# An SSM convolution and a 16-expert MoE in one kernel: coefficients computed between the steps of a series, loads and small VectorE work moved behind the first heads

## The chip, the cores and the metric

The kernel runs on one NeuronCore of a Trainium2 chip. The metric is the device time of one execution in microseconds (us); less is better. Three executions of the kernel before took 910.34, 914.94 and 912.26 us, so their median is 912.26 us. A further execution, the profiled one, gave every row that is quoted here.

## The reference, cut to what matters

`x` has shape (128, 32, 512): 128 batches, 32 heads `h`, 512 positions `l`. A diagonal state-space model with 64 states per head gives each head a convolution kernel:

```
dt = exp(log_dt);  A = -exp(log_A_real) + i*A_imag;  dtA = A*dt
Ct = C * (exp(dtA) - 1) / A
K[h, l] = 2 * Re( sum_n Ct[h, n] * exp(dtA[h, n] * l) )
y = (causal convolution of x with K over l) + x*D, set to 0 where l >= length[batch]
```

`y` has 4096 rows (batch, head) of 512. A router (sigmoid of a 16-column product, plus bias) takes 4 of 16 experts for each row. Each expert is a gated unit, `silu(y Wg) * (y Wu)` times `Wd`, with 256 inner columns; a shared expert of the same size works on every row. The output is `x` plus all of it.

## The kernel before, in words

**The head of the program.** Everything begins with `Ct` and the waves `exp(dtA*l)`. `exp_into` (L273) makes `dn = exp(logs)`, that is `dt` and `nar = exp(log_A_real)`, in 32 columns. `waves` (L303) makes the magnitude `mag` by a polynomial (`exp_parts`, L258: the six dependent steps of L269 are "the series") and cosine and sine on ScalarE, for one chunk of states. There are six chunks (`CHUNKS`, L281); (c0, n) covers heads 2*c0 to 2*(c0+n)-1. L342 to L374 then form `Ct` as `ct_r`, `ct_i` by small VectorE operations of 16 columns: `er + i*ei = exp(dtA) - 1` (L344 to L349), `C` times that (L353 to L358), divided by `A` (L361 to L374). `kernels` (L379) multiplies waves and `Ct` into factors (the last one is L403), lets TensorE turn them into a chunk's kernel rows (`pk`, L407), adds the skip term (`krow`, L415) and writes them to DRAM (`kd`, L421 and L422). `kernel_strip` (L427) reads them back as a Toeplitz matrix, the `strip` of a block of four heads, 1 MB.

**The convolutions.** `tb` numbers eight blocks of four heads. In the loop at L998 TensorE convolves head 0, head 1, and then two heads at a time (`convolve`, L602, products at L610), with x read as `xt` (1 MB a block, L155, two buffers). How much of the sequence the longest row lets it leave out is read from `skips` by TensorE's sequencer ahead of heads 2 and 3 (L625). VectorE masks each result into `yb` (L628), ScalarE's queue writes a block of `yb` to `y_rows` in DRAM (L1006), TensorE turns it into `yT` (L634). `behind_head` (L954) puts the other work behind each head: waves of chunk 1 and 2 after heads 0 and 1, kernels of chunk 1 after head 0, of chunk 2 after head 3, of chunk 3 after head 8. The router's `gates`, `sums` and `route` follow each block or second block.

**Order.** In this stage TensorE's order is the one written in the program; that of VectorE, ScalarE, GpSimd and of the SyncE queue (which issues nearly all loads) is found by the scheduler from priorities and dependencies, `dep(a, b)` adding a dependency by hand. Ahead of head 0 TensorE runs eight matmuls that only keep it busy (L446), the ranking of rows by length (L496, L498, from `longer`, L493), and eight more; `rank`, `to_rank` and `to_row` (L503 to L508) are read from that PSUM result.

**From 121 us on** every engine's order is written in the program. Eight units run through the shared expert (`w_sh`, the last 3072 columns of `store`; L1071, L1086), then tiles of routed rows through the experts (L1211, L1237). Behind the last unit's third `down`, `registers(0)` and `registers(1)` (L1148, L1149) load two registers each on TensorE (L1202, L1205).

Of the kernel before, what the change touches and what calls it, by code (L numbers as in the profile page):

```python
# [28 lines left out]
F32 = mybir.dt.float32  # L29
BF16 = mybir.dt.bfloat16  # L30
F16 = mybir.dt.float16
I32 = mybir.dt.int32
AF = mybir.ActivationFunctionType
ALU = mybir.AluOpType
# [4 lines left out]
P = 128  # L39
# [17 lines left out]
AHEAD = 4  # L57
NT = (B * H * TOPK - E) // P + E
NT_MIN = B * H * TOPK // P
LAST_DRAIN = NT_MIN - 4  # L60
TS = 64
SKIPS = 4
# [17 lines left out]
def ssm_moe_kernel(  # L80
# [71 lines left out]

    def load_xt(tb):
        t = xp.tile([P, KT, HB, P], F32, tag="x", name=f"xt{tb}")
        nc.sync.dma_start(out=t, in_=x_t[tb])  # L155
        return t

    def dep(of, on, why):
# [88 lines left out]
    def ptile(name):  # L247
        return const.tile([P, NC2], F32, tag=name, name=name)

    def reduce_angle(r, k):  # L250
# [4 lines left out]
            nc.vector.scalar_tensor_tensor(r, k, -part, r, ALU.mult, ALU.add)  # L255
        nc.vector.tensor_scalar(r, r, -math.pi, math.pi, ALU.max, ALU.min)

    def exp_parts(v, q, k, s):  # L258

        nc.vector.tensor_scalar(v, v, -87.0, 88.0, ALU.max, ALU.min)
        nc.vector.tensor_scalar(k, v, 1.0 / math.log(2.0), ROUND, ALU.mult, ALU.add)
        nc.vector.tensor_scalar(k, k, ROUND, None, ALU.subtract)
        for part in (LN2_1, LN2_2):
            nc.vector.scalar_tensor_tensor(v, k, -part, v, ALU.mult, ALU.add)
        nc.vector.tensor_scalar(q, v, SERIES[0], None, ALU.mult)
        for c in SERIES[1:]:
            nc.vector.scalar_tensor_tensor(q, q, c, v, ALU.add, ALU.mult)  # L269

        nc.vector.tensor_scalar(s, k, 127.0, 2.0**23, ALU.add, ALU.mult)
# [67 lines left out]

    first, (mag, q, s, r, half) = waves(*CHUNKS[0], NC2)  # L340

    t0, t1, t2, t3 = (ptile(f"t{i}") for i in range(4))  # L342
    ex, em1, er, ei = mag[:, :NC2], ptile("em1"), ptile("er"), ptile("ei")
    nc.vector.tensor_mul(t1, q[:, :NC2], s[:, :NC2])  # L344
# [3 lines left out]
    nc.vector.tensor_add(er, t0, em1)  # L348
    nc.vector.tensor_mul(ei, ex, r[:, :NC2])  # L349

    c_r, c_i = cc[:, 0, :], cc[:, 1, :]
    nr, ni = ptile("nr"), ptile("ni")
    nc.vector.tensor_mul(t0, c_r, er)  # L353
    nc.vector.tensor_mul(t1, c_i, ei)
    nc.vector.tensor_sub(nr, t0, t1)
    nc.vector.tensor_mul(t0, c_r, ei)
    nc.vector.tensor_mul(t1, c_i, er)
    nc.vector.tensor_add(ni, t0, t1)  # L358

    rd, m0, m1 = ptile("rd"), ptile("m0"), ptile("m1")  # L360
    nc.vector.tensor_mul(m0, nar, nar)  # L361
    nc.vector.tensor_mul(m1, aim, aim)
    nc.vector.tensor_add(m0, m0, m1)
    nc.vector.reciprocal(rd, m0)
    nc.vector.tensor_mul(t0, ni, aim)
    nc.vector.tensor_mul(t1, nr, nar)
    nc.vector.tensor_sub(t0, t0, t1)
    nc.vector.tensor_mul(t2, ni, nar)
    nc.vector.tensor_mul(t3, nr, aim)
    nc.vector.tensor_add(t2, t2, t3)  # L370

    ct_r, ct_i = ptile("ct_r"), ptile("ct_i")
    nc.vector.scalar_tensor_tensor(ct_r, t0, 2.0, rd, ALU.mult, ALU.mult)
    nc.vector.scalar_tensor_tensor(ct_i, t2, 2.0, rd, ALU.mult, ALU.mult)  # L374


    kd_of, strip = {}, {}

    def kernels(c0, n, mag, cos, sin):  # L379

# [19 lines left out]
        nc.vector.tensor_add(g_r, g_r, g_t)  # L400
        nc.vector.tensor_mul(g_i, e_r, by_i)
        other.tensor_mul(e_i, e_i, by_r)
        nc.vector.tensor_sub(g_i, g_i, e_i)  # L403
        pk = ps_m.tile([P, n, 2 * LB], F32, tag="m", name=f"pk{c0}")
        for c in range(n):
            for g, f in ((g_r, f_r), (g_i, f_i)):
# [17 lines left out]
            kd_of[h] = kd[h - 2 * c0 : h - 2 * c0 + 1, :]  # L424
        return last

    def kernel_strip(tb):  # L427
        s = ks1.tile([P, HB, L], F32, tag="strip", name=f"strip{tb}", bufs=2)

        each = 1 if tb == 0 else HB  # L430
        for q in range(0, HB, each):
            kd = kd_of[tb * HB + q]
            nc.sync.dma_start(
                out=s[:, q : q + each, :],
                in_=bass.AP(kd.tensor, kd.offset, [[1, P], [PAD + L, each], [1, L]]),
            )
        strip[tb] = s

# [35 lines left out]


    len_col = const.tile([P, 1], F32, tag="len_col", name="len_col")
    behind(nc.vector.tensor_copy(len_col, len_col_i))
    key_row = const.tile([P, B], F32, tag="key_row", name="key_row")
    behind(nc.vector.tensor_copy(key_row, len_row_i))
    key_col = const.tile([P, 1], F32, tag="key_col", name="key_col")  # L480
    longest = const.tile([1, 1], F32, tag="longest", name="longest")
    for key, raw, own in ((key_row, key_row, cpos), (key_col, len_col, ppos)):
        nc.vector.tensor_scalar(key, raw, 0.0, float(L), ALU.max, ALU.min)
        if key is key_row:
            nc.vector.tensor_reduce(longest, key[0:1, :], AX.X, ALU.max)
        if key is key_col:
            num_len = const.tile([P, 2], F16, tag="num_len", name="num_len")
            behind(nc.vector.tensor_copy(num_len[:, 0:1], ppos))
            nc.vector.tensor_copy(num_len[:, 1:2], key)
        nc.vector.scalar_tensor_tensor(key, key, float(P), own, ALU.mult, ALU.subtract)  # L490

    longer = const.tile([P, B], BF16, tag="longer", name="longer")
    nc.vector.tensor_scalar(longer, key_row, key_col, None, ALU.is_lt)  # L493
# [10 lines left out]

    to_rank = const.tile([P, P], F32, tag="to_rank", name="to_rank")
    nc.vector.tensor_scalar(to_rank, cpos, rank, None, ALU.is_equal)
    to_row = const.tile([P, P], F32, tag="to_row", name="to_row")
    nc.vector.tensor_scalar(to_row, rank_ps[:, :B], ppos, None, ALU.is_equal)  # L508

    of_ranks = {}  # L510

    def ranks():
# [3 lines left out]
        def later(op):  # L516
            dep(op, last_mask, "later in VectorE's order")

        to_rank_h = const.tile([P, P], F16, tag="to_rank_h", name="to_rank_h")
        later(nc.vector.tensor_copy(to_rank_h, to_rank))  # L520
        unit = const.tile([P, NU], BF16, tag="unit", name="unit")
        later(nc.vector.tensor_scalar(unit, upos, 0.0, None, ALU.is_equal))

# [53 lines left out]


    skips = const.tile([1, 1], I32, tag="skips", name="skips")
    nc.vector.tensor_scalar(longest, longest, -1.0, float(L), ALU.mult, ALU.add)  # L580
    floor_div(longest, longest, TS)
    nc.vector.tensor_scalar(skips, longest, float(SKIPS - 1), None, ALU.min)


    within = const.tile([P, L], F32, tag="within", name="within")
# [363 lines left out]
    weights_at = {19: 0, 27: 1}  # L949
    made_waves, strips, k_us = {}, [1], {}  # L950
    ybs, xbs, rest_of_ranks = {}, {0: load_xt(0)}, ranks()
    nc.sync.dma_start(out=w_sh, in_=w_all[E])

    def behind_head(h):  # L954

        tb, q = divmod(h, HB)
        if h in waves_at:
            made_waves[waves_at[h]] = waves(*waves_at[h], 0)[0]
        if h in kernels_at:
            c = kernels_at[h]  # L960
            chunk_last[c[0]] = kernels(*c, *made_waves[c])
            behind_masks(chunk_last[c[0]])

        if strips[-1] in (tb, tb + 1) and strips[-1] < NB and strips[-1] * HB in kd_of:
            kernel_strip(strips[-1])
            strips.append(strips[-1] + 1)
        if h in (22, 25, 29):
            next(rest_of_ranks, None)
        if h in weights_at:
            weights_out(weights_at[h])  # L970
        if q == 2 and tb > 0:
            gates(tb - 1)
        last = h == H - 1
        for each in turns_at(h):
            turn_y(each, ybs[each // HB])
        if q == 3 and tb > 0 and not last:
            sums_and_route(tb - 1)
        if last:

            sums_and_route(tb - 1)  # L980
            k_us[0] = nc.tensor.value_load(of_ranks["k_u"][0:1, 0:1], min_val=1, max_val=KT)
            turned = turn_y(h, ybs[tb])
            gates(tb)
            return turned
# [12 lines left out]
    with tc.manual_schedule(engines={mybir.EngineType.PE}):  # L997
        for h, n in [(0, 1), (1, 1), *((h, 2) for h in range(2, H, 2))]:  # L998
            tb, q = divmod(h, HB)
            if q == 0:  # L1000
                ybs[tb] = yp.tile([P, HB, L], F32, tag="yb", name=f"yb{tb}")
                if tb + 1 < NB:
                    xbs[tb + 1] = load_xt(tb + 1)
            convolve(tb, range(q, q + n), xbs[tb], ybs[tb])
            if q + n == HB:
                nc.scalar.dma_start(out=y_bh[:, tb * HB : (tb + 1) * HB, :L], in_=ybs[tb])  # L1006
            for each in range(h, h + n):
                turned = behind_head(each)

# [106 lines left out]
    def unit_step(u):  # L1116
# [20 lines left out]
        for q in range(TU // P):  # L1137
            if u > 0 and not (u == NU and q == TU // P - 1):
                down(u - 1, q)
                if q % 2 == 1:  # L1140
                    next(making, None)
                if q == 0 and u + 1 < NU:
                    unit_register(u + 1)
            if u == NU - 1 and q == TU // P - 2:
                for _ in making:
                    pass

                registers(0)  # L1148
                registers(1)  # L1149
                registered = True  # L1150
        while "get" in made and gathered < AHEAD:
            gather(gathered)
            gathered += 1
# [225 lines left out]
```

## Time and profile before

| | us |
|---|---|
| median of three runs | 912.26 |
| the profiled execution | 913.3 |
| span of its core, first to last instruction | 911.5 |
| around the span (the difference) | 1.8 |
| TensorE busy | 871.8 |
| VectorE busy | 414.5 |
| first product of head 0 | 23.11 |
| first matmul of the shared expert | 121.53 |
| first routed product | 268.23 |

A row of the timeline has the start, the duration, the engine (PE is TensorE, PEld its weight load, DVE VectorE, ACT ScalarE, POOL GpSimd, SPq and ACTq the DMA-issuing queues), the line, the operation, what is written from what, and in brackets how long the engine sat idle before it and what released it. The chain of waits is the path that ended last: start, length, who. A row of a window has its length, the busy time of PE, PEld, DVE, ACT and POOL with their counts, then the granted TensorE clock (1.00 is full), the busy share of the DMA engines and their GB/s. A span of an operation on VectorE is longer than the distance to the next one where the two overlap; the chain shows the distance.

### The profile page before, as it was taken

The page shows a single profiled execution, that of the slowest core. Times are in us where ns is not written, and L with a number is a line of the kernel's source. Part 1 is how long each engine was busy: PE and PEld are TensorE (multiplying, and loading weights), DVE is VectorE, ACT ScalarE, POOL GpSimd, SP SyncE. Part 2 cuts the span into 40 slices and gives each one's busy share as a digit, 9 for nine tenths or more (in the row PEclk, how much of TensorE's full clock was granted, in tenths as well). Part 3 has the DMA queues.
Part 4 walks back from the last instruction along what each step waited for, and adds up shares of the span by engine and source line. Part 5 has one row for each costly group of instructions (what it writes and reads, how often), then busy time and mean ns, then how long its engine had stood idle before and what let it go on. Part 6 is the DMA issues. An engine that isn't in the chain of part 4 may idle for free.

```text
span 911.5 us, 14694 instructions
## 1 busy us (share of the span) xinstructions
PE 871.8 (96%) x2976; PEld 445.1 (49%) x2976; DVE 414.5 (45%) x1488; ACT 188.6 (21%) x379; POOL 421.7 (46%) x372
## 2 busy tenths in 40 slices
PE   2999999999999999999999999999999999999992
PEld 1667754444445444445444544444444554444440
DVE  8977774878712334323342334333333233344331
ACT  1222221112221122212221122112221111222220
POOL 2210012323574556555664556555654445566462
PEclk9999999999999999999999999999999999999997
DMA  5677586786696767666676667566765656677573
GB/s 200 211 269 257 198 276 181 220 179 163 101 218 168 179 118 130 132 165 118 120 138 169 110 117 138 111 106 118 133 115 99 107 107 107 110 139 132 106 131 75
DMA packets 54710, 136.03 MB, mean 149 GB/s; under 512 B 12432, under 2 KB 12592, under 8 KB 50992
## 3 DMA queue, kind: packets, MB, share of 16 engines
q0 software_dynamic: 36256, 89.77, 53.9%
q1 hardware_dynamic: 14096, 36.15, 11.3%
q10 hardware_dynamic: 4224, 8.39, 2.5%
q8 instruction: 76, 1.25, 0.5%
q14 instruction: 58, 0.48, 0.2%
HBM read 288.08 MB, written 60.64 MB: 383 GB/s over the span
## 4 chain that ended last, share of the span: by engine, by line
PE 91%; DVE 4%; DMA 1%; issue 1%; POOL 0%; ACT 0%; SPq 0%; DVEq 0%; ACTq 0%; POOLq 0%
PE g L1211 35%; PE o L1237 25%; PE py L610 6%; PE o L1086 5%; PE m L1179 5%; PE g L1071 4%; PE u L1071 4%; PE u L1229 3%; PE pt L634 1%; PE pa L901 1%; PE parts L655 1%; DMA strip<-kd 1%; PE pg L672 1%; DVE wq L269 0%; DVE pick L834 0%
## 5 line engine op out<-in xcount | busy, mean ns | idle before, releaser
L1211 PE MATMUL g<-store,yt 128*128 x742 | 342.9, 595 | 1.5 <-issue 1.1
L1247 POOL DMA_INDIRECT out<-ob,put x134 | 209.8, 1566 | 228.4 <-DVE junk L1186 204.1
L1237 PE MATMUL o<-store,zT 128*128 x536 | 252.0, 592 | 0.0
L1223 DVE SCALAR_TENSOR_TENSOR zt<-g,wt,sgt 128x256 f32<-128x256 f32 x135 | 65.3, 484 | 302.8 <-ACT sgt L1222 302.8
L1211 PEld LDWEIGHTS g<-store,yt 128*128 128x128 f32 x742 | 130.3, 190 | 118.2 <-issue 117.4
L1036 POOL DMA_INDIRECT yg<-y_rows,get x140 | 142.1, 1015 | 49.6 <-issue 38.6
L1237 PEld LDWEIGHTS o<-store,zT 128*128 128x128 f32 x536 | 101.5, 190 | 128.7 <-issue 124.1
L1246 DVE COPY ob<-o 128x512 f32<-128x512 f32 x134 | 92.7, 692 | 109.2 <-PE o L1237 100.2
L1185 ACT COPY yt<-m 128x512 f32<-128x512 f32 x136 | 79.6, 585 | 225.9 <-PE m L1179 219.7
L1222 ACT ACTIVATE sgt<-g 128x256 f32<-128x256 f32 x135 | 51.8, 383 | 267.2 <-PE g L1211 267.2
L1095 POOL DMA_INDIRECT out<-ob,unit_rows x32 | 50.0, 1563 | 93.0 <-ACT ob L1093 59.8
L1179 PEld LDWEIGHTS m<-ident,yg 128*128 128x128 f32 x373 | 48.7, 141 | 72.2 <-issue 71.7
L610 PE MATMUL py<-strip,xt 128*128 128x192 f32 (+7 forms) x256 | 63.6, 403 | 1.2 <-DMA strip<-kd 1.2
L1179 PE MATMUL m<-ident,yg 128*128 128x128 f32 x373 | 63.1, 273 | 0.8 <-issue 0.6
L1086 PE MATMUL o<-store,z 128*128 128x512 f32 x128 | 58.0, 597 | 0.7 <-ACT ob L1093 0.7
L1232 DVE COPY zT<-u 128x256 f32<-128x256 f32 x134 | 56.4, 421 | 1.3 <-PE u L1229 1.3
L610 PEld LDWEIGHTS py<-strip,xt 128*128 128x128 f32 x256 | 44.4, 195 | 19.6 <-issue 12.8
L1229 PE MATMUL u<-ident,zt 128*128 128x128 f32 x268 | 51.2, 273 | 0.0
L1071 PE MATMUL g<-store 128*128 128x512 f32 x92 | 42.8, 600 | 0.5 <-PE parts L655 0.3
L913 DVE TENSOR_SCALAR cols<-tpos_h,stl,tok 128x143 f16<-128x143 f16 x128 | 42.3, 336 | 0.0
L1071 PE MATMUL u<-store 128*128 128x512 f32 x92 | 42.2, 593 | 0.0
L1086 PEld LDWEIGHTS o<-store,z 128*128 128x128 f32 x128 | 23.4, 190 | 26.5 <-issue 24.9
(285 smaller groups left out, 493.1 us busy)
## 6 DMA issues: line engine op xcount, KB each, us to landing
store<-in_w_all SPq DMA_DIRECT2D x143, 1536.0 KB
xt<-in_x_t SPq DMA_DIRECT2D x8, 1024.0 KB
y_rows<-yb ACTq DMA_DIRECT2D x8, 1024.0 KB
out<-in_x POOLq DMA_DIRECT2D x8, 1024.0 KB, 15.7
strip<-kd SPq DMA_DIRECT2D x7, 1024.0 KB
yg<-y_rows,get POOLq DMA_INDIRECT x140, 4.4
out<-ob,put POOLq DMA_INDIRECT x134, 4.9
strip<-kd SPq DMA_DIRECT2D x4, 256.0 KB
```

The lines of the kernel that those rows point to most:

```text
L610: nc.tensor.matmul(py[:, c0 : L - jt * P], lhsT=xt[:, jt, q, :], rhs=strip[tb][:, q, jt * P + c0 :], start=(jt == 0), stop=(jt == KT - 1 o ...
L1036: nc.gpsimd.indirect_dma_start(out=at(yg, t), out_offset=None, in_=y_rows[:, :], in_offset=bass.IndirectOffsetOnAxis(ap=made["get"][:, t : ...
L1071: nc.tensor.matmul(ps[it], lhsT=w_sh[:, c0 : c0 + P], rhs=yT[:, u, kt, :, :].rearrange("p h b -> p (h b)"), start=(kt == KT - n), stop=(kt ...
L1086: nc.tensor.matmul(po, lhsT=at(zu, u)[:, it, q * P : (q + 1) * P], rhs=w_sh[:, c0 : c0 + L], start=(it == 0), stop=(it == IT - 1),)
L1179: nc.tensor.transpose(pt[:, q, :], at(yg, t)[:, q * P : (q + 1) * P], ident)
L1185: nc.scalar.copy(at(yt, t), pt)
L1211: mm = nc.tensor.matmul(pgu, lhsT=at(yt, t)[:, q, :], rhs=ring_flat[:, bass.ds(w0s[t] + q * 2 * I, 2 * I)], start=(q == KT - n), stop=(q = ...
L1223: nc.vector.scalar_tensor_tensor(at(zs, t), pgu[:, I:], at(wts, t), sg, ALU.mult, ALU.mult)
L1229: nc.tensor.transpose(at(p_z, t)[:, it, :], at(zs, t)[:, it * P : (it + 1) * P], ident)
L1237: mm = nc.tensor.matmul(po, lhsT=at(zts, t)[:, it, :], rhs=ring_flat[:, bass.ds(w0s[t] + WD + it * L, L)], start=(it == 0), stop=(it == IT ...
L1246: nc.vector.tensor_copy(ob, po)
L1247: add = nc.gpsimd.indirect_dma_start(out=out, out_offset=bass.IndirectOffsetOnAxis(ap=made["put"][:, t : t + 1], axis=0), in_=ob, in_offse ...
```

## The change

1. `Ct` is regrouped. The coefficient `ca` (2 C / A up to sign and conjugation: `ca_r`, `ca_i`) is formed from `nar`, `aim` and `cc` alone, by twelve operations that stand in the program between the first waves and `er`; three of them wait for the first operation of the waves' series, so that they and what follows from them fall among its steps. After `er` and `ei` six operations are left (four products, one sum, one difference).
2. The second block of x (`tb == 1`) waits for the last of block 0's four strip loads.
3. The shared expert's weights `w_sh` are no longer loaded (1.5 MB) at the start by SyncE's queue, but in six pieces of 256 KB on ScalarE's queue, each behind the y_rows write of blocks 1 to 6 and behind the same mask.
4. The length keys are formed in four operations instead of six, behind chunk 0's last factor (L403) instead of behind its `krow`; `num_len`'s two casts go to the first part of `ranks()` (behind head 22).
5. `skips` is found behind chunk 1's last factor.
6. `to_row` is no longer made from PSUM on the spot: ScalarE copies the rank row to SBUF and VectorE makes `to_row` behind head 10.
7. `registers(0)` goes behind the last unit's second `down`, `registers(1)` stays behind the third.

```
     def load_xt(tb):
...
+        load = nc.sync.dma_start(out=t, in_=x_t[tb])
+        if tb == 1:
+            dep(load, first_strips, "behind what is wanted first")
...
+    def between(op):
+        dep(op, in_series, "between the series' steps, of which each waits for the one ahead")
+
+    between(nc.vector.tensor_mul(m0, nar, nar))
+    nc.vector.tensor_mul(m1, aim, aim)
+    nc.vector.tensor_add(m0, m0, m1)
+    nc.vector.reciprocal(rd, m0)
+    nc.vector.tensor_mul(ca_r, c_i, aim)
+    between(nc.vector.tensor_mul(m1, c_r, nar))
+    between(nc.vector.tensor_mul(ca_i, c_i, nar))
+    nc.vector.tensor_mul(m2, c_r, aim)
+    nc.vector.tensor_sub(ca_r, ca_r, m1)
+    nc.vector.tensor_add(ca_i, ca_i, m2)
+    nc.vector.scalar_tensor_tensor(ca_r, ca_r, 2.0, rd, ALU.mult, ALU.mult)
+    nc.vector.scalar_tensor_tensor(ca_i, ca_i, 2.0, rd, ALU.mult, ALU.mult)
...
+    nc.vector.tensor_mul(t0, ca_r, er)
+    nc.vector.tensor_mul(t1, ca_i, ei)
+    nc.vector.tensor_mul(t2, ca_i, er)
+    nc.vector.tensor_mul(t3, ca_r, ei)
+    nc.vector.tensor_add(ct_r, t0, t1)
+    nc.vector.tensor_sub(ct_i, t2, t3)
...
+    for key, raw in ((len_col, len_col_i), (key_row, len_row_i)):
+        op = nc.vector.tensor_scalar(key, raw, 0.0, float(L), ALU.max, ALU.min)
+        dep(op, factors_last[0], "later in VectorE's order")
+    nc.vector.scalar_tensor_tensor(key_col, len_col, float(P), ppos, ALU.mult, ALU.subtract)
+    nc.vector.scalar_tensor_tensor(key_row, key_row, float(P), cpos, ALU.mult, ALU.subtract)
...
+    nc.scalar.copy(rank_row, rank_ps[:, :B])
     to_row = const.tile([P, P], F32, tag="to_row", name="to_row")
-    nc.vector.tensor_scalar(to_row, rank_ps[:, :B], ppos, None, ALU.is_equal)
...
+    def find_skips(after):
+
+        longest = const.tile([1, 1], F32, tag="longest", name="longest")
+        op = nc.vector.tensor_reduce(longest, key_row[0:1, :], AX.X, ALU.max)
+        dep(op, after, "later in VectorE's order")
+        nc.vector.tensor_scalar(longest, longest, -1.0, float(L * P), ALU.mult, ALU.add)
+        floor_div(longest, longest, TS * P)
+        nc.vector.tensor_scalar(skips, longest, float(SKIPS - 1), None, ALU.min)
...
-    nc.sync.dma_start(out=w_sh, in_=w_all[E])
+    first_strips = strip_loads[-1]
...
+            if h == 0:
+                find_skips(factors_last[c[0]])
...
+        if h == TO_ROW_AT:
+            to_row_op = nc.vector.tensor_scalar(to_row, rank_row, ppos, None, ALU.is_equal)
+            behind_masks(to_row_op)
...
                 nc.scalar.dma_start(out=y_bh[:, tb * HB : (tb + 1) * HB, :L], in_=ybs[tb])
+                if 1 <= tb <= PIECES:
+
+                    own = slice((tb - 1) * WSZ // PIECES, tb * WSZ // PIECES)
+                    load = nc.scalar.dma_start(out=w_sh[:, own], in_=w_all[E][:, own])
+                    dep(load, masks[-1], "behind what is wanted first")
...
-            if u == NU - 1 and q == TU // P - 2:
+            if u == NU - 1 and q in (1, 2):
                 for _ in making:
                     pass
 
-                registers(0)
-                registers(1)
-                registered = True
+                registers(q - 1)
+                registered = q == 2
```

`PIECES` is 6 and `TO_ROW_AT` is 10.

## The prediction, made before the changed kernel was built or run

> **What bounds the kernel now.** I read the page's busy row first, then the chain of waits, then the timelines of TensorE and of SyncE's queue for the stretch up to 121 us, then the half-second windows where TensorE stands still.
>
> ```profile
> PE 871.8 (96%) x2976; PEld 445.1 (49%) x2976; DVE 414.5 (45%) x1488; ACT 188.6 (21%) x379; POOL 421.7 (46%) x372
> ```
>
> TensorE is busy 96% of 911.5 us. From 268 us on it multiplies with hardly a gap, and the change touches nothing there. Of the 39.7 us without a matmul 16 lie ahead of the first one and some 15 behind the last, so only a few are left between. Where is it?
>
> ```profile
> 17.28 3.57 PE L446 MATMUL py<-ones 128*128 128x512 bf16 x8 [0.40 <-DVE krow L415]
> 23.11 2.32 PE L610 MATMUL py<-strip,xt 128*128 128x512 f32 x8
> 26.48 0.22 PE L407 MATMUL pk<-f_r,gg_r 128*32 128x32 f32 x2 [1.05 <-DVE gg_r L400]
> 34.08 0.25 PE L407 MATMUL pk<-f_r,gg_r 128*32 128x32 f32 x2 [0.71 <-DVE gg_r L400]
> 59.15 5.57 PE L610 MATMUL py<-strip,xt 128*128 128x448 f32 x16 [1.23 <-DMA strip<-kd]
> 260.39 1.98 PE L1086 MATMUL o<-store,z 128*128 128x512 f32 x4 [0.69 <-ACT ob L1093]
> ```
>
> TensorE's timeline: the first real work is at 15.96, the first product of head 0 at 23.11; then come four holes, of 1.05, 0.71, 1.23 and 0.69 us. Head 0 doesn't wait for its strip: the keep-busy matmuls and the ranking fill 17.28 to 23.11 and TensorE takes them in order. What starts them is `krow`, and the chain ahead of `krow` is VectorE alone, from 4.07 us on. In it the series looks like this (chain of waits; start, length):
>
> ```profile
> 11.11 0.29 DVE wq L269
> 11.39 0.02 issue
> 11.42 0.28 DVE wq L269
> 11.69 0.09 DVE t L346
> 11.78 0.23 DVE wq L269
> ```
>
> One step to the next takes 0.31 us (11.11 to 11.42). With a 16-column operation (L346) between two of them the timeline's next step starts at 11.73, again 0.31 later: the filler was free.
>
> **The change, part by part.** The sum is made against the profiled execution: 913.3 us, 911.5 of span and 1.8 around it, which is 1.0 above the median of 912.26.
>
> *`Ct` regrouped.* Eighteen operations before, eighteen after; only the place counts. (a) Ahead of the waves the chain has L361 0.09, L363 0.09, an issue of 0.02 and the reciprocal L364 0.25. All leave: -0.45. (b) Behind the series, from L344 (12.31) to the first factor L398 (15.32), stand 25 operations in 3.01 us, 0.12 each. Fourteen leave (L353 to L358, L365 to L370, L373, L374), six come: -8 x 0.12 = -0.96. (c) Nine operations go among the main series' steps; the other three depend on inputs alone and fit among the steps of `dn`'s series, as L362 does at 4.68. The main series has six gaps of 0.31 - 0.18 = 0.13 (0.18 is the distance from L266 to an operation that doesn't depend on it), two already taken by L271 and L346. Five find room there or behind the last step, four don't: 4 x 0.09 = +0.36, of which I take 0.30. Net -1.10.
> The Trainium skill speaks against (c): "VectorE: DVE Perf Modes", section "The DRAIN you can't avoid", says the next operation does not start until the pipe is empty, and so to cut the count of operations. By that each of the nine costs its 0.17 and 0.02 of issue, +1.7, and the whole is +0.3, a loss. The row at 11.69 differs (0.09 and no delay of the next step), so I take -1.10 and keep +0.3 as the other end.
>
> *Small VectorE work out of the stretch from `krow` to chunk 1's factors* (17.17 to 26.34). By start-to-start distance: casts L477 0.07 and L479 0.13, `num_len` 0.14, `to_row` 0.26 and the keys (L483, L490, L493) 0.68 leave it, the keys into the 0.62 in which VectorE waits for `pk`; skips' operations (L485 to L582) 0.46 go behind it. Together 1.7, more than the hole of 1.05 at 26.48. But VectorE also reads `rank` in this stretch (it stood 0.41 for it, L503), and that comes 3.7 behind the start of keep-busy whatever VectorE does; if the scheduler leaves `rank` at the same place in the order, up to 1.5 turns into waiting there and 0.2 is left. Ends -1.05 and -0.2; I take -0.8, since a scheduler that knows the wait can put series steps ahead of it. The hole of 0.71 at 34.08 stays: its factors follow head 1's mask (L628, 29.33), which moves with TensorE.
>
> *Moved work that I cost at nothing, with its cover.* `skips`: six operations, 1.1 us as a chain (0.20 and five of 0.18), behind chunk 1's factors; TensorE's sequencer wants it 2.2 behind the present factors, and a mask of 0.6 may come between: no margin to speak of, 0 to +0.5, taken 0. The rank row's copy on ScalarE: it idles 11.2 ahead of L329 at 22.17; behind it waits only that sine. `to_row` behind head 10: 0.26 among masks, wanted at 82. The six pieces: six issues of 0.37 to 0.42 on ScalarE's queue, each behind a y_rows issue with the same mask, so no new wait; behind them stand the yT copies (L635), with 3.4 to 6.8 of idle time in most rows. The sixth goes out near 111.7 and takes 0.7 at 370 GB/s; it is wanted at 121.5. Between 77 and 103 the DMA engines are full; there the mask of head 20 (89.06) waited 2.9 for a y_rows write and has 0.85 left until head 23 needs its PSUM: 0 to +0.7, taken 0. The 1.5 MB that vanish from the start (DMA full from 9 to 17.2) make `kd` and the strips up to 2 us earlier, but head 0 waits for the keep-busy matmuls: 0.
>
> *Registers.* One pair takes 1.3 us of TensorE's sequencer (257.6 to 258.9); two are 2.6 against the 1.72 of one `down`, hence the 0.69 at 260.39. Split, each lies behind a `down`: -0.65.
>
> Sum: 1.10 + 0.80 + 0.65 = 2.55. The strip hole stays: chunk 3's `pk` is not late (49.76, factors done at 45.8), and what follows (`kd` 50.96, strip 52.89, landed 59.1) moves as a whole. 912.26 - 2.55 = 909.7 us.
>
> **The rivals.**
>
> *R1, slower: x's second block is in the way of the second strip.* SyncE's queue shows what an x block does to the next small write:
>
> ```profile
> 28.98 0.39 SPq L433 DMA_DIRECT2D strip<-kd  x1
> 32.95 0.36 SPq L155 DMA_DIRECT2D xt<-in_x_t  x1
> 35.09 0.33 SPq L422 DMA_DIRECT2D kd<-krow  x1
> 39.73 0.37 SPq L433 DMA_DIRECT2D strip<-kd  x1
> ```
>
> `kd` was written in 1.42 at 27.56 (to 28.98), but in 4.64 at 35.09, two us behind an x block. After the change x's second block goes out near 22 and chunk 1's `kd` near 25.7. If that took 4.64, strip 1, which now lands near 34 with about 1.2 to spare, would come 2.0 too late at heads 4 and 5. And such a hole costs twice:
>
> ```profile
> 59.00:59.50 0.50, 0.35 (x1) 0.30 (x2) 0.47 (x4) 0.00 (x0) 0.43 (x1) 1.00 1.03 377
> 59.50:60.00 0.50, 0.50 (x2) 0.29 (x1) 0.47 (x2) 0.00 (x0) 0.37 (x2) 0.54 1.09 410
> 62.00:62.50 0.50, 0.50 (x5) 0.50 (x3) 0.50 (x4) 0.00 (x0) 0.00 (x0) 0.50 0.99 381
> 63.00:63.50 0.50, 0.50 (x2) 0.19 (x1) 0.35 (x2) 0.00 (x0) 0.00 (x0) 1.00 1.05 410
> ```
>
> Behind the 1.23 of idle time the granted clock is 0.50 for some 3.2 us, and sixteen matmuls take 5.57 instead of 3.62: +1.95. So 2.0 + 1.95 - 2.55 = +1.4: 913.7. It starts to cost when `kd` takes over 2.6 and cancels the gain at about 3.2. Against it: at 35.09 a strip's tail and a y_rows write (35.27) were under way as well, while from 24 to 30 the engines are idle (share 0.03), so that 1 MB at 420 GB/s is through by about 26.
>
> *R2: the gaps are not free* (the drain rule holds): +0.3 - 0.8 - 0.65 = -1.15: 911.1.
>
> *R3: `rank` takes the freed time*: -1.10 - 0.2 - 0.65 = -1.95: 910.3.
>
> *R4: the half clock falls away.* "TensorE: Matmul & The Clock Gate", part "The HAM clock gate", lets the clock fall after an idle window of about 3.4 us and calls the window free-running. Here 1.23 us of idle time sufficed, and 1.05 at 26.48 did not. If the place in such a window decides, a shift of 2 us can save the 1.95, or put it on another hole; by the page no hole of this size costs it at all. I keep it where it is, as the trace has it: -2.55 - 1.95 gives 907.8.
>
> *R5: the pieces or `skips` cost what I put at nothing*: +0.7: 910.4.
>
> **How the numbers follow.** Forecast 0.47, R1 0.12, R2 0.11, R3 0.11, R4 0.12, R5 0.07. Likeliest is 909.7; the cases span 907.8 to 913.7, and single runs of the kernel before scatter by 2.7 around their median, so the range is 907.0 to 913.5. What a measurement of this kernel can tell from no change is about 0.5%, 4.6 us. Faster by more (under 907.7) needs R4 with all the rest: 0.16. Slower by more (over 916.8) needs R1 and a second loss: 0.05. Within: 0.79.
>
> **What would show it.** `krow` L415 at 15.8 instead of 16.92; head 0's first product at 22.0; the hole at chunk 1's `pk` under 0.3; heads 4 and 5 at about 33.2 instead of 35.01 with no wait for a strip; a strip hole of 1.2 and a half clock behind it near 57; no hole behind the last `registers`; the first routed product at 265.7 instead of 268.23. Steps of over 0.31 in the series speak for R2, a long wait at L503 for R3, a strip wait ahead of heads 4 and 5 for R1. I'm wrong if anything behind 121 us other than the registers changes its length, or if a DMA wait opens between 77 and 103.

## The result: 914.57 us against 912.88, slower by a quarter per cent

Beside each other on one chip the changed kernel took 914.57 us (median of 21 executions, 912.76 to 916.68) and the kernel before 912.88 (21 executions, 910.32 to 917.05). The ratio is 1.0024 with a 95% interval of 1.0014 to 1.0033: about 2 us slower (1.7 by the medians), where I had forecast 2.55 us faster. That lies above the range of 907.0 to 913.5, and above the worst of my cases, 913.7, which the range should have taken in. Both profiled executions are near their medians: 913.7 us with a span of 912.0 after, 913.3 with 911.5 before.

TensorE's timeline of the changed kernel, the rows that answer to those of before (keep-busy, head 0, the kernel rows of chunks 1 and 2, heads 4/5, heads 12/13, heads 24/25, the last `down`s):

```profile
16.26 3.06 PE L460 MATMUL py<-ones 128*128 128x512 bf16 x8 [0.40 <-DVE krow L425]
...
21.12 2.42 PE L630 MATMUL py<-strip,xt 128*128 128x512 f32 x8
23.47 0.25 PE L417 MATMUL pk<-f_r,gg_r 128*32 128x32 f32 x2
...
30.60 0.22 PE L417 MATMUL pk<-f_r,gg_r 128*32 128x32 f32 x2 [0.27 <-DVE gg_r L410]
...
33.95 3.89 PE L630 MATMUL py<-strip,xt 128*128 128x448 f32 x16 [2.07 <-DMA strip<-kd]
...
60.15 5.30 PE L630 MATMUL py<-strip,xt 128*128 128x448 f32 x16 [3.19 <-DMA strip<-kd]
...
97.09 3.86 PE L630 MATMUL py<-strip,xt 128*128 128x448 f32 x16 [0.99 <-DMA strip<-kd]
...
255.94 7.03 PE L1116 MATMUL o<-store,z 128*128 128x512 f32 x16
```

The three holes that the change aimed at are gone or small: none at chunk 1's `pk` (1.05 before), 0.27 at chunk 2's (0.71), none among the last `down`s (0.69). In their place stand three waits for a strip: 2.07, 3.19 and 0.99 us, where before there was one of 1.23. The last of them, at 97.09, is the DMA wait between 77 and 103 that I had named as a sign of being wrong. Set side by side, the start of the same work in the two profiled executions:

| first matmul of | before | after | difference |
|---|---|---|---|
| head 0 | 23.11 | 21.12 | -1.99 |
| chunk 1's `pk` | 26.48 | 23.47 | -3.01 |
| chunk 2's `pk` | 34.08 | 30.60 | -3.48 |
| heads 4 and 5 | 35.01 | 33.95 | -1.06 |
| heads 12 and 13 | 59.15 | 60.15 | +1.00 |
| heads 24 and 25 | 95.53 | 97.09 | +1.56 |
| shared expert | 121.53 | 123.08 | +1.55 |
| last instruction | 911.5 | 912.0 | +0.5 |

So 3.5 us had been won by 31 us, of which about one is chance. In this execution the sixteen keep-busy matmuls took 4.86 us (16.26 to 21.12), where they took 5.83 before. In e1 below, which has the same program up to 40 us, they took 5.86:

```profile
16.23 3.57 PE L461 MATMUL py<-ones 128*128 128x512 bf16 x8 [0.40 <-DVE krow L426]
...
22.09 2.32 PE L631 MATMUL py<-strip,xt 128*128 128x512 f32 x8
```

Of the 3.5 us, 2.4 were lost at heads 4/5, 2.1 more at heads 12/13, and half a microsecond up to heads 24/25. Behind 123 us some 1.05 came back, of which 0.69 is the hole of the registers.

The wait at heads 12/13 has a half clock behind it again. In the half-microsecond windows (the clock is the third number from the end):

```profile
59.50:60.00 0.50, 0.00 (x0) 0.00 (x0) 0.50 (x2) 0.00 (x0) 0.42 (x2) 0.63 1.09 455
62.50:63.00 0.50, 0.50 (x3) 0.30 (x2) 0.00 (x0) 0.00 (x0) 0.00 (x0) 0.50 1.02 397
63.00:63.50 0.50, 0.50 (x6) 0.50 (x4) 0.00 (x0) 0.00 (x0) 0.00 (x0) 0.96 1.07 418
```

TensorE stands still in the first, runs at 0.50 in the second and is back at 0.96 in the third. Sixteen matmuls took 5.30 us; the next sixteen, at full clock, took 3.79.

### The profile page after: what moved, and what is told of

Same layout as the page of the kernel before. It is cut to its first block, busy times and chain, and to the rows that moved or that the text cites. A ratio compares the mean times of both kernels' runs of the same rounds, so it can differ in the third digit from the quotient of the medians.

```text
span 912.0 us, 14707 instructions
## 1 busy us (share of the span) xinstructions
PE 871.0 (96%) x2976; PEld 444.4 (49%) x2976; DVE 412.8 (45%) x1486; ACT 189.4 (21%) x380; POOL 422.7 (46%) x372
```

## Where strip 3 lost its time

Heads 12/13 need strip 3. Its `krow` is written to DRAM and read back by SyncE's queue; SyncE's timeline of the changed kernel:

```profile
50.00 0.32 SPq L432 DMA_DIRECT2D kd<-krow  x1
51.54 0.37 SPq L446 DMA_DIRECT2D strip<-kd  x1
```

The strip's load goes out 1.35 us earlier than before (51.54 against 52.89), as it should. But the first matmul that it feeds starts 8.6 us later, where it took 6.3 before. What is new beside it shows on ScalarE's queue. First the kernel before, then the changed one:

```profile
44.92 1.07 ACT L635 COPY store<-pt 128x512 f32<-128x512 f32 x2
45.41 0.37 ACTq L1006 DMA_DIRECT2D y_rows<-yb  x1
```

```profile
43.96 1.07 ACT L655 COPY store<-pt 128x512 f32<-128x512 f32 x2
50.12 0.59 ACT L655 COPY store<-pt 128x512 f32<-128x512 f32 x1 [5.09 <-PE pt L654]
50.18 0.37 ACTq L1031 DMA_DIRECT2D y_rows<-yb  x1
50.59 0.52 ACTq L1035 DMA_DIRECT2D store<-in_w_all  x1
```

Before, the write of block 1's y_rows (1 MB) is issued among the two copies of head 5's turn, at 45.41. After, the scheduler has put it behind the first copy of the next block, which waits 5.09 us for TensorE; so it goes out at 50.18, with the first piece of `w_sh` behind it, 1.4 us ahead of the strip. Its data were there at about 43: nothing that it needs is late, only its place in the order is. What that does to the DMA engines is plain in the 1 us windows (the last two numbers are their busy share and GB/s), here with the changed kernel first and then e4 below, in which neither load is moved and block 1's write goes out at 44.33:

```profile
51.00:52.00 1.00, 1.00 (x6) 0.73 (x5) 1.00 (x6) 0.59 (x1) 0.00 (x0) 1.00 0.97 349
52.00:53.00 1.00, 1.00 (x6) 0.63 (x6) 1.00 (x5) 0.00 (x0) 0.00 (x0) 1.00 1.05 373
```

```profile
51.00:52.00 1.00, 1.00 (x7) 0.84 (x6) 1.00 (x6) 0.07 (x1) 0.00 (x0) 1.00 0.00 0
52.00:53.00 1.00, 1.00 (x6) 0.63 (x5) 1.00 (x6) 0.00 (x0) 0.00 (x0) 1.00 0.27 80
```

In e4 the strip finds idle engines at 51.5; after the change it has to share them. The experiments ask whether this write is the cause, or one of the two moved loads itself.

## The experiments

Each is the changed kernel with the edit shown. Ratios are to the kernel before on the same chip, with the 95% interval; "above e4" is the difference of two such ratios. e1 to e4 ran on one chip, e5 to e8 on a second, e9 to e12 on a third. Holes are those of the one profiled execution, and by chance alone they differ by about 1 us: at heads 4/5 e6 waited 2.22 and e12, with the same program up to there, 1.24.

**e4: both loads as before.** Computation, small operations and registers changed; x's second block without its wait, `w_sh` whole at the start on SyncE's queue.

```
-        if tb == 1:
-            dep(load, first_strips, "behind what is wanted first")
...
+    nc.sync.dma_start(out=w_sh, in_=w_all[E])
...
-                if 1 <= tb <= PIECES:
...
```

> The changed kernel with both loads as before: only the computation, the small VectorE work, the copy on ScalarE and the registers are changed. All theories: the wait at heads 24 and 25 goes, strip 3's is 1.2 to 1.5. Theory C: heads 4 and 5 wait less than 0.8. Then about 910 to 910.5, 2.5 us under the kernel before; if the computation's gain is eaten by strip 1's own chain all the same, 911.5.

909.25 us, ratio 0.9981 (0.9967 to 0.9995). TensorE's timeline:

```profile
22.68 2.40 PE L628 MATMUL py<-strip,xt 128*128 128x512 f32 x8 [0.26 <-DMA strip<-kd]
...
33.82 3.89 PE L628 MATMUL py<-strip,xt 128*128 128x448 f32 x16 [1.00 <-DMA strip<-kd]
...
57.09 3.89 PE L628 MATMUL py<-strip,xt 128*128 128x448 f32 x16 [0.25 <-DMA strip<-kd]
```

So the computation is worth what I forecast to within the measurement, and the two load edits together cost 1.0024 - 0.9981 = 0.43%, some 3.9 us. Two more things stand in these rows. Head 0 waits 0.26 for its strip, which it does not where the loads are moved; the rest of the distance to 21.12 lies in the pace of the keep-busy matmuls. And heads 4/5 are at 33.82 here and at 33.95 there: nothing of the earlier start arrives.

**e3: no pieces, x's wait kept.** `w_sh` is loaded at the start as in e4.

```
+    nc.sync.dma_start(out=w_sh, in_=w_all[E])
...
-                if 1 <= tb <= PIECES:
...
```

> The changed kernel with the shared expert's weights loaded whole at the start by SyncE's queue, as before; x's second block still waits for the strips, and block 1's y_rows write still stands behind the yT copy. Theory A: strip 3 is still 2.2 us or more late, since 1 MB of the 1.25 MB in its way is left; the new wait at heads 24 and 25 (0.99) goes; about 913.3. Rival B: strip 3's wait falls to 1.2 to 1.5 and the one at heads 24 and 25 goes: about 911.6.

912.17 us, ratio 1.0009 (0.9997 to 1.0021). Block 1's write is at 49.66, still displaced; 1.27 at heads 4/5, 2.35 at heads 12/13, none at 24/25. The write is late in the two kernels that have the wait of x's second block (this one and the changed one), and early in e2 and e4, which have not. So it is the dependency of x's second block, on SyncE's queue, that makes the scheduler order ScalarE's queue differently.

**e2: pieces kept, x's wait taken away.**

```
-        load = nc.sync.dma_start(out=t, in_=x_t[tb])
-        if tb == 1:
-            dep(load, first_strips, "behind what is wanted first")
+        nc.sync.dma_start(out=t, in_=x_t[tb])
```

> The changed kernel with x's second block loaded at the start again, without the wait for the strips; the pieces stay. In this program the scheduler puts block 1's y_rows write at its former place by itself. If x's second block delays chunk 1's kernel rows and strip 1 (theory C), the wait of heads 4 and 5 falls from 2.07 us to 0.8 or less, and with it the write back in place takes 1.6 to 2 off strip 3's wait: about 911.5. If C is wrong, the wait of heads 4 and 5 stays at 1.7 to 2.1 (strip 1 limited by its own chain), and the time is about 912.8.

913.02 us, ratio 1.0008 (0.9992 to 1.0024). Block 1's write is back at 45.88 by itself; yet heads 4/5 wait 1.55, heads 12/13 2.06, heads 24/25 2.34, each with a half clock behind it (this execution took 917.78, 4.8 above the median). The ratio is 0.27% above e4's, with intervals that just overlap; e5 below shows more clearly that the pieces cost something of their own.

**e1: both loads moved, the order on ScalarE's queue mended.** An ordering without a wait puts the copy behind block 1's write.

```
+            copy = turn_y(each, ybs[each // HB])
+            if q == 0 and tb == 2:
+                tc.add_manual_dep(copy.ins, y_out[1].ins.name, ORDER, reason="in ScalarE's order")
```

> The changed kernel with one thing more: block 1's y_rows write, which ScalarE's queue issued behind a yT copy that waited for TensorE until 50.1 us, is ordered (without a wait) ahead of that copy again, as in the kernel before. Everything else of the change stays, the six pieces and the wait of x's second block too. Theory A (the order of ScalarE's queue: that write, 1 MB, and the piece behind it fell on the load of strip 3): the wait of heads 12 and 13 for strip 3 goes from 3.19 us to 1.2 to 1.6, and the time falls by 1.5 to 2 us, to about 912.8. Rival B (the pieces themselves are in the way of the strips): the wait stays at 2.5 or more and the time within 0.5 us of the changed kernel's 914.6.

913.20 us, ratio 1.0014 (1.0001 to 1.0028). The write is at 43.83, the first piece at 44.24; 1.17 at heads 4/5, 1.78 at 12/13, 1.37 at 24/25, a half clock behind the last two. That is 0.1% below the changed kernel, with intervals that overlap, so that the order alone helps is not shown while the pieces remain. It is 0.33% above e4.

**e5: the order mended and no pieces** (e1 and e3 together).

> The kernel of e3 (weights whole at the start, x's second block still behind the strips), with block 1's y_rows write ordered ahead of the yT copy as in e1. Theory A (what the wait of x's second block costs is the place of that write in ScalarE's queue, which the scheduler changed with it): the write starts near 44, the wait for strip 3 falls from 2.35 us to 0.3 to 1.2, and the kernel comes to e4's time, 909.3 to 910, a ratio to the kernel before of 0.998 to 0.999. Rival (the load of x's second block itself, in the way of chunk 1's kernel rows and of what follows): the time stays at e3's ratio of 1.0009.

910.29 us, ratio 0.9981 (0.9969 to 0.9993), the same as e4. So the wait of x's second block costs nothing by itself; what it cost in e3 came from the place of the write. And as e1 differs from e5 by the pieces alone, they cost 0.33% (0.9969 to 0.9993 against 1.0001 to 1.0028). (The profiled execution took 914.98, 4.7 above the median, with 2.36 and 1.78 of waiting; its rows don't stand for the median.)

**e9: e4 with block 1's write put late, and nothing else.** Neither load is moved.

```
+            if h == 8:
+                y1 = nc.scalar.dma_start(out=y_bh[:, HB : 2 * HB, :L], in_=ybs[1])
+                tc.add_manual_dep(y1.ins, copy.ins.name, ORDER, reason="in ScalarE's order")
...
+                if tb != 1:
+                    nc.scalar.dma_start(out=y_bh[:, tb * HB : (tb + 1) * HB, :L], in_=ybs[tb])
```

> e4 (both loads as before) with one thing more: block 1's y_rows write issued behind the yT copy that the changed kernel put ahead of it. Theory A says that this place alone carries what the wait of x's second block cost: the write starts near 50, strip 3 is waited for 2 us or more instead of 0.25, and the ratio to the kernel before goes from e4's 0.9981 to e3's 1.0009 (1.000 to 1.0015). Rival: strip 3 is limited by its own chain and e4's profile was a lucky one; then the ratio stays under 0.9990.

913.26 us, ratio 1.0020 (1.0004 to 1.0036): 0.39% above e4 from one DMA issued 6 us later. Its TensorE row:

```profile
59.32 5.28 PE L629 MATMUL py<-strip,xt 128*128 128x448 f32 x16 [2.20 <-DMA strip<-kd]
```

2.20 in place of e4's 0.25, with the strip issued at the same time (51.68 against 51.55). So a late write alone is enough to lose nearly all that the two load edits lost. It is not the only thing that is enough: the pieces without a late write (e2, e1) lose most of it too.

**e10 and e11: which pieces.** Both are e2 with another split: in e10 pieces 1 and 2 behind blocks 1 and 2 and the other four in one load behind block 6; in e11 three pieces behind blocks 3, 4, 5 and the other half behind block 6.

```
-PIECES = 6
+PIECES = {1: (0, 1), 2: (1, 2), 6: (2, 6)}
...
```

```
-PIECES = 6
+PIECES = {3: (0, 1), 4: (1, 2), 5: (2, 3), 6: (3, 6)}
...
```

> e2 (x's second block at the start, six pieces, ratio 1.0008) with only the first two pieces at their places, behind blocks 1 and 2, and the other four sixths in one load behind block 6. If the pieces cost through strip 3 (heads 12 and 13, piece 1 beside it), the ratio stays at 1.0005 or more; if through strip 6 (heads 24 and 25, pieces 3 to 5 in the full stretch from 77 us), it falls to e4's 0.9981 to 0.9990, and no wait at heads 24 and 25 is left.

914.44 us, ratio 1.0025 (1.0013 to 1.0036); 2.31 at heads 4/5, 1.99 at 12/13, none at 24/25. It also loses time around 120 us, where block 7's order differs:

```profile
121.03 1.75 PE L673 MATMUL parts<-store,gw 128*32 128x512 f32 x8 [0.68 <-ACT store L653]
123.08 4.47 PE L1099 MATMUL g<-store 128*128 128x512 f32 x8 [0.31 <-PE parts L673]
```

From block 7's last convolution to the shared expert it takes 7.12 us (115.96 to 123.08) where e4 takes 5.44, and the eight matmuls behind it run in part at half clock (0.50 from 122 to 124 us), 4.47 instead of 3.69. Together that is some 2.5 of the 4 us that it lies above e4.

> The complement of e10: pieces of one sixth behind blocks 3, 4 and 5, the other half behind block 6, none behind blocks 1 and 2. If strip 6 carries the cost: heads 24 and 25 wait 1 to 2.3 us for it and the ratio is 1.000 to 1.001; if strip 3 does: 0.9981 to 0.9990, and strip 3 is waited for no more than in e4 or e6 (0.25 to 0.5).

911.37 us, ratio 0.9996 (0.9984 to 1.0008); 1.79 at heads 4/5, 0.89 at 12/13, 0.35 at 24/25. That is 0.15% above e4, with intervals that overlap. Which pieces are the dear ones does not follow from the two ratios: less its 2.5 us around 120 us, e10 would by my estimate be at about 0.9998, beside e11. Only strip 3's holes (1.99 and 0.89) point to the first two.

**e6: the weights in one load on SyncE's queue, behind block 6's last mask**; x as before.

```
+                if tb == LATE_AT:
+                    load = nc.sync.dma_start(out=w_sh, in_=w_all[E])
```

> The computation of the change, x's second block at the start, and the shared expert's weights in one load of 1.5 MB on SyncE's queue behind the mask of heads 26 and 27, where the DMA engines of the kernel before are idle from 103 to 111 us. If the pieces cost by lying beside the strips (A and B agree), no strip but the first ones is waited for by more than in e4, and the time is e4's or less: less by up to 0.5 us, since the start is free of 1.5 MB and head 0 need not wait for its strip (0.26 in e4): 908.5 to 909.3. If moving those weights anywhere behind the start costs, 911 or more.

910.60 us, ratio 0.9978 (0.9966 to 0.9989). Issued at 105.79, where the DMA engines are no longer full, the load costs nothing to be seen. Heads 4/5 wait 2.22 all the same, heads 12/13 0.47.

**e7: e6 with `skips` found behind chunk 1's `krow`** instead of behind its factors, to let that `krow` go first.

```
-                find_skips(factors_last[c[0]])
+                find_skips(chunk_last[c[0]])
```

> e6, and skips found behind chunk 1's kernel rows (krow) instead of behind its last factor. In the changed kernel those six operations and a mask stand ahead of krow on VectorE (krow at 25.85, two us behind its matmuls at 23.9). If that is what makes strip 1 late, krow comes 0.5 to 1 us earlier, the wait of heads 4 and 5 falls from 1.0 us to 0.3 or less, and the time by 0.5 to 1 us; if TensorE then waits for skips ahead of heads 2 and 3, it gives the same back: no change against e6.

911.66 us, ratio 0.9990 (0.9976 to 1.0004), no gain. `krow` comes no earlier: 25.82, 2.18 behind its last matmul (23.64), where the changed kernel has 2.17. The scheduler put other steps of the next waves in the free places. TensorE now waits for `skips`, though the row names another releaser (heads 2/3 start 1.52 behind the operation that writes `skips`, at 27.47 here and at 27.66 in e8):

```profile
28.99 5.48 PE L628 MATMUL py<-strip,xt 128*128 128x448 f32 x16 [2.77 <-DVE ge_r L402]
```

**e8: e7 with chunk 3's kernels behind head 7 instead of 8.**

```
-    kernels_at = dict(zip((0, 3, 8, 14, 20), CHUNKS[1:]))
+    kernels_at = dict(zip((0, 3, 7, 14, 20), CHUNKS[1:]))
```

> e7, and chunk 3's kernels made behind head 7 instead of behind head 8 (its factors are ready 4 us before TensorE gets to them). Its kernel rows and strip 3 come up to 4 us earlier, so the hole ahead of heads 12 and 13 and the half clock behind it can't arise: against the kernel before (hole 1.23 and 1.95 of half clock) 3 us less than e7 where e7 still has the hole, nothing where it has not. 906 to 908.

911.51 us, ratio 0.9990 (0.9979 to 1.0001). No strip wait is left, but the hole at heads 2/3 is (2.76).

**e12: e6 with chunk 3 behind head 7.**

> e6 (weights in one late load, x's second block at the start, skips where the change has them) with chunk 3's kernels behind head 7, as in e8. In e7 and e8 TensorE stood 2.8 us ahead of heads 2 and 3, where skips came late; that is undone here. Strip 3's hole can't arise; what is left are strip 1 and its half clock. Against e6 (0.9978): 0.9965 if strip 3's hole still cost something there on average, the same 0.9978 if not.

909.69 us, ratio 0.9974 (0.9962 to 0.9986). Heads 4/5 wait 1.24, chunk 3's `pk` 0.16 and 0.35, heads 12/13 no longer. It beats both kernels; from e4, e5 and e6 it can't be told apart.

**One table for strip 3.** From the profiled executions: when block 1's write and chunk 3's `kd` were issued, and how long it was from that `kd` to the first matmul of heads 12/13.

| kernel | pieces 1, 2 | write of block 1 | `kd` | `kd` to strip's issue | strip's issue to matmul | sum | idle | ratio |
|---|---|---|---|---|---|---|---|---|
| e4 | no | 44.33 | 49.87 | 1.68 | 5.54 | 7.22 | 0.25 | 0.9981 |
| e6 | no | 46.99 | 52.53 | 1.56 | 5.88 | 7.44 | 0.47 | 0.9978 |
| e11 | no | 44.16 | 49.71 | 1.62 | 6.23 | 7.85 | 0.89 | 0.9996 |
| before | no | 45.41 | 50.96 | 1.93 | 6.26 | 8.19 | 1.23 | 1 |
| e5 | no | 46.65 | 52.20 | 1.84 | 6.90 | 8.74 | 1.78 | 0.9981 |
| e1 | yes | 43.83 | 49.42 | 2.14 | 6.60 | 8.74 | 1.78 | 1.0014 |
| e10 | yes | 44.68 | 50.22 | 2.49 | 6.46 | 8.95 | 1.99 | 1.0025 |
| e2 | yes | 45.88 | 51.42 | 2.55 | 6.47 | 9.02 | 2.06 | 1.0008 |
| e9 | no | 50.34 | 50.16 | 1.52 | 7.64 | 9.16 | 2.20 | 1.0020 |
| e3 | no | 49.66 | 49.48 | 1.52 | 7.79 | 9.31 | 2.35 | 1.0009 |
| after | yes | 50.18 | 50.00 | 1.54 | 8.61 | 10.15 | 3.19 | 1.0024 |

(e7 is left out, since TensorE stood still in it at heads 2/3; e8 and e12 place the chunk elsewhere.) The sum less the idle time is 6.96 to 6.97 in every row: that is TensorE's own work between chunk 3's `kd` and heads 12/13. So the hole is the length of this chain less 6.96. With a late write and no pieces the strip's load is about 2 us longer than e4's (e9, e3). With the first two pieces and an early write the chain is 1.5 to 1.8 longer than e4's, a third to a half of it ahead of the strip's issue; why there, with the engines nearly idle from 50 to 53 us in e1, the traces didn't tell me. With both the chain is 2.9 longer.

Each row is one execution, and not all are typical: those of e4, e9 and e11 took 1.3 to 2.3 us less than their medians, those of e1, e2 and e5 1.6 to 4.8 more. e5, with neither a piece nor a late write, has e1's sum. So the table shows where the time goes, and not how much of a row is chance; what the edits cost is told by the ratios.

## Why the prediction was wrong, step by step

**Right: `Ct` regrouped.** -1.10 forecast; `krow` came at 15.90 instead of 16.92, -1.02, although `logs` landed 0.13 later. Part (b), from `wm` to chunk 0's factor, took 2.30 instead of 3.25: -0.95 for my -0.96. Part (c), the nine operations among the steps, is to be read on VectorE's timeline after:

```profile
10.23 0.27 DVE L275 SCALAR_TENSOR_TENSOR wq<-wq,wv 128x112 f32<-128x112 f32 x1
10.41 0.17 DVE L356 TENSOR_TENSOR m<-dn 128x16 f32<-128x16 f32 x1
10.50 0.17 DVE L362 TENSOR_TENSOR ca_i<-cc,dn 128x16 f32<-128x16 f32 x1
10.58 0.27 DVE L275 SCALAR_TENSOR_TENSOR wq<-wq,wv 128x112 f32<-128x112 f32 x1
```

With two fillers a step takes 0.35 instead of 0.31. From the first step to `wm` it is 2.05 instead of 1.85: +0.20 for my +0.30, and not the +1.7 of the drain rule. R2 falls. I had quoted that rule without the end of its paragraph: "VectorE: DVE Perf Modes", "The DRAIN you can't avoid", adds that a next operation that is not held starts earlier. These rows agree (0.09 from one 16-column operation to the next), so the page did not speak against (c).

**Right: VectorE's small work and the registers.** The 1.05 at chunk 1's `pk` is gone altogether (-0.80 forecast), R3 with it; the hole of 0.71 shrank to 0.27, which I had not counted; the 0.69 is gone. e4, with these parts alone, gives -0.19% where my whole sum of -2.55 is -0.28%: inside its interval. Head 0 came at 22.09 in e1, with the keep-busy matmuls at their pace of before, where I had said 22.0.

**Wrong, the step that decided: "what follows (`kd` 50.96, strip 52.89, landed 59.1) moves as a whole", and of the pieces "each behind a y_rows issue with the same mask, so no new wait".** I treated the distance from `kd` to the landed strip as fixed. It contains two transfers, and by the table it runs from 7.22 to 10.15 with what lies beside them. My sum left the hole at 1.23; it became 3.19, and half a clock stayed behind it. The two load edits, which I had put at 0, cost 0.43%, some 3.9 us, more than the whole gain of 2.55. Two mechanisms: I costed moved issues by what stands behind them in their queue and never asked what the scheduler does to another queue's order when it replans (e3, e9: 0.28 and 0.39% above e4); and I asked what delays the pieces, not what the pieces delay (e1 against e5: 0.33%; this is R5, which I had put at +0.7 at most and had looked for between 77 and 103 us). Together they cost 0.43%, less than their sum. That fits, as both stretch the chain to strip 3, but that this chain is all of it is argued.

**Wrong place, right suspicion: R1.** A wait at heads 4/5 did open, 2.07, and it took 2.4 us of what had been won. The delay that I had feared was there too: chunk 1's `kd` took 1.71 to 2.89 in the four kernels in which x's second block waits (2.45 in the changed one), and 1.41 to 1.46 in all the others. But it did not decide. Without the wait of x's block heads 4/5 wait 0.86 to 2.31 (e2, e4, e6, e9 to e12), with it 1.17 to 2.36 (e1, e3, e5, after), since without it strip 1's load takes 5.3 to 6.8, with it 5.3 to 5.4. I had expected heads 4/5 at 33.2 with strip 1 in time. Strip 1 has its own chain, from chunk 1's `krow`, and VectorE's timeline after shows that this has not moved as far as TensorE has:

```profile
25.08 0.67 DVE L648 TENSOR_TENSOR yb<-py,within 128x512 f32<-128x512 f32 x1
25.85 0.21 DVE L425 TENSOR_TENSOR krow<-pk,dsk 32x64 f32<-32x64 f32 x1
```

Its last matmul starts at 23.68, yet `krow` comes at 25.85, behind `skips`, the waves of the next chunk and a mask. Then `kd` takes 2.45 and the strip 5.4. The 1.05 in front of `pk` had been won; VectorE work now stands in front of `krow`, 2.17 us where it was 0.61 before (26.71 to 27.32). Moving `skips` away (e7) did not shorten it, since steps of the waves took the place. Whether less work ahead of this `krow` would win the 2 us was tried in no other way, so that it would is argued and not shown.

**"The 1.5 MB that vanish ... : 0".** Nearly right. With `krow` 1 us earlier and the loads as before, head 0 waited 0.26 (e4) and 0.76 (e9) for its strip; with x's block or the weights moved it waited in no run. But heads 4/5, which wait for a strip of their own, took that back.

**R4: the half clock is a matter of chance, and between 1.2 and 2.3 us the length of a hole doesn't decide it.** Of the holes of 1 us and more at the convolutions in the profiled executions, those of 1.00, 1.17, 1.24, 1.27, 1.47, 1.79, 2.07 and 2.31 us left the clock at full; those of 1.23, 1.37, 1.55, 1.78, 1.99, 2.06, 2.20, 2.22 and all from 2.34 on halved it. So up to some 2.3 us the length doesn't tell. That fits a free-running window, which the Trainium skill states ("TensorE: Matmul & The Clock Gate", "The HAM clock gate"), but an idle time of 3.4 us isn't needed for it. The half clock also goes with most of the scatter. On the chip of e1 to e4, 40 of 51 executions of the kernel before had a mean granted clock of 0.993 or more and a median of 911.2 us, 11 had 0.992 or less and 914.2. So the profiled execution of before, 913.3 us at 0.991 with a half clock at 59 us, is like the 11: "as the trace has it" was not the usual case. e4 has 13 of 22 in the upper group, with a median of 908.7, 2.5 below; of the changed kernel's 21 executions none is in it. More and longer holes make the half clock nearly sure.

**Open.** Of the 1.05 us that come back behind 123 us, 0.36 isn't traced, so something behind 121 us other than the registers did change its length. What each piece costs is not settled, nor how piece 1 lengthens the time from `kd` to the strip's issue.

## What to carry to other kernels

Where a scheduler finds the order, a dependency added on one queue can move an instruction on another: compare the order of every queue after such an edit, and look for transfers that were ready and go out late. A load that nobody waits for still costs when it lies beside one that TensorE waits for, so put it where the DMA engines are idle (here, issued at 105.79, it cost nothing to be seen). And when a stall is removed, follow the next transfer's chain from its first instruction, since work taken out of the way of one consumer can stand in the way of the next. One profiled execution of each kernel differs by chance as much as such an edit is worth: read where the time goes from it, and what an edit costs from many executions.

## What the runs showed of the hardware that I had not expected

One 1 MB write issued 1.3 us ahead of a strip's load lengthened it from 5.5 to 7.6 us (e4, e9), though the two are on different queues. A load can stand in ScalarE's queue for long: the fourth piece of the weights went out 5.8 us after its y_rows write (83.84 and 89.65 in the changed kernel), where the five others took 0.4. And the sixteen keep-busy matmuls at the start, the same in every kernel, took 4.86 us in the changed kernel and 5.86 in e1, with a granted clock of 1.00 in the rows of both.
